# Graph layers on one core: marks for GpSimd written by ScalarE, the transposed mask taken as a sign, and two layernorm steps placed later

## The chip, the cores and the metric

The kernel runs on one core of one Trainium2 chip. The core has five engines that work side by side, each through its own queue in order: TensorE (PE, its weight loads shown as PEld), VectorE (DVE), ScalarE (ACT), GpSimd (POOL) and SyncE (SP), which issues DMAs. They wait for each other through semaphores. The metric is the device time of one execution in microseconds (us), lower is better.

## What is computed

The reference takes 16 graphs of 1024 nodes with 64 channels, a weighted adjacency matrix of 1024 x 1024 for each (its pattern of edges symmetric, about 16 neighbours in a row), and runs four layers with a layernorm and a ReLU ahead of each and a residual sum after it:

```python
h = relu(layernorm(x));  x = x + (tanh([h, adj @ h] @ W1 + b1) @ W2 + b2)        # layer 0
h = relu(layernorm(x));  x = x + ((adj + I) @ h) / (rowsum(adj) + 1)             # layer 1
h = relu(layernorm(x));  x = x + gin(h + quantiles(h, dilate(adj)))              # layer 2
h = relu(layernorm(x));  x = x + ((adj @ h) / colsum(adj)) @ Wn + h @ Ws + b     # layer 3
```

`dilate` drops from each row with more than 10 neighbours every skip-th one (counted along the row by a running sum), and the same edges in the transposed place; `quantiles` takes, per node and channel, a weighted sum of the 25%, 50% and 75% quantiles of the values of the neighbours that are left.

## The kernel before

Each graph goes through six streams of work, written as generators: `adjacency` (load rows, compare with zero, transpose, dilate, build a key per neighbour), `layers` (layers 0 and 1, the layernorm of layer 2), `neighbour_lists` (the columns of each node's neighbours, by repeated maxima), `gathers` (neighbours' rows of h into `raw`), `sorts` (a sorting network over `raw`, then the weighted sums) and `tail` (rest of layer 2, layer 3, output). Different graphs stand in different streams at the same time.

*The order of the work* is written by hand. A `Clock` carries planned times for VectorE, TensorE, ScalarE and GpSimd. A generator issues some instructions, adds their planned cost, and yields the planned time from which it wants to go on; the loop at the end of `direct_path` goes on with the first stream, in a fixed order of priority, whose time has come on VectorE's planned clock. So what is yielded sets only the place of the next instructions in each engine's queue. `after(dve, pe, act, lat)` adds the costs, ScalarE's after TensorE's after VectorE's, and gives back the end plus `lat`.

*Gathers and gates.* `gathers` (L1233 on) issues on GpSimd, per graph, 124 indirect DMAs (L1275), each of 128 rows of h, in five groups; each is planned at 1.39 us. At every fourth one it calls `gate()` and yields `clk.pool - 5`. `gate` (L914), if VectorE's planned clock is 3 us past the last mark, has VectorE write a mark (a memset of one element, L917), and GpSimd copy it (L919). GpSimd thereby waits for all that VectorE has in its queue up to there. A sort of a group (L1308) waits for its gathers; gathers into a group's buffer wait until the graph before has sorted it.

*The mask.* In `adjacency` each block of 128 rows is compared with zero (L942, `nb`, in f16, its diagonal taken out in L944) and is also transposed by TensorE into `adjt` (L949, L950), f32, which holds the whole transposed matrix with its diagonal. `flipped(i)` (L975) transposes `nb` once more, eight 128 x 128 tiles on TensorE into a PSUM bank of a ring of three (`bank()`), and ScalarE copies it out (L980). Running counts are products of that tile with a staircase (L991); ScalarE takes an absolute value (L995) and VectorE a comparison (L1000, L1005), which gives `gone`.

*Layernorm.* `preln` (L843) is called four times a graph. VectorE subtracts the mean, ScalarE squares (L851), VectorE sums the squares (L853), ScalarE takes the root (L854), VectorE the reciprocal (L856) and the product (L857), ScalarE the ReLU (L858). The places of L853 and L856 in VectorE's order come from the `lat` of the calls of `after` at L852 and L855, 1.2 and 1.5 us.

*Messages.* `messages` (L871) multiplies `adjt` with h, 32 products of 512 columns (L877), and ScalarE copies the result out (L878). In layer 1, eight ScalarE copies of `adjt` in place (L1212) follow, which sum it up for layer 3. The plan has 10.5 us of TensorE for the first (L1187) and 14.0 for the second (L1216), 1.1 us of ScalarE after each.

A flag of graphs that this path can't take (`bad`, L1455 on) sends all to another path; with these inputs it isn't taken.

Of the kernel before, what the change touches and what calls it, by code (L numbers as in the profile page):

```python
# [19 lines left out]
NB = 8  # L20
# [28 lines left out]
BIG = 1e30  # L49

E_ID, E_ONE, E_CAP, E_LOW, E_CN, E_HALF, E_Q, E_END = 0, 128, 256, 264, 272, 280, 288, 352
J_ID, J_BIG, J_OFF, J_ST, J_ROW, J_ONE, J_PI, J_NI, J_END = 0, 128, 256, 384, 896, 1920, 2048, 2176, 2184

# [678 lines left out]
def direct_path(ctx: ExitStack, tc: tile.TileContext, t: dict, out: bass.AP, flag):  # L732
# [17 lines left out]
    tt, ts, act = nc.vector.tensor_tensor, nc.vector.tensor_scalar, nc.scalar.activation  # L750
# [4 lines left out]
    ch = const.tile([P, J_END], F16, name="eh")  # L755
    nc.scalar.dma_start(ch, t["eh"])
    identf, onesf = cf[:, E_ID:E_ID + P], cf[:, E_ONE:E_ONE + P]
    cap8, low8, cn8, half8 = (cf[:, e:e + NB] for e in (E_CAP, E_LOW, E_CN, E_HALF))
    identh, big_i, offdiag = (ch[:, e:e + P] for e in (J_ID, J_BIG, J_OFF))
    stair, pidx = ch[:, J_ST:J_ST + N // 2], ch[:, J_PI:J_PI + P]  # L760
    nid = ch[:, J_NI:J_NI + NB]
    jrow, onerow = ch[0:1, J_ROW:J_ROW + N], ch[0:1, J_ONE:J_ONE + P]
    eps = const.tile([P, 1], F32, name="eps")
    nc.vector.memset(eps, 1e-5)
    bad = const.tile([P, NB], F32, name="bad")
    nc.vector.memset(bad, 0.0)

    def weight(name, n):
        w = const.tile([n, t[name].shape[1]], F32, name=name)
# [45 lines left out]

    clk = Clock()

    def after(dve=0.0, pe=0.0, act=0.0, lat=0.3):

        clk.dve += dve  # L820
        at = clk.dve
        if pe:
            clk.pe = at = max(clk.pe, at) + pe
        if act:
            clk.act = at = max(clk.act, at) + act
        return at + lat


    def bank(dt=F32):
        return psum.tile([P, 2048 // mybir.dt.size(dt)], dt, tag="t", name="pt", bufs=3)  # L830
# [12 lines left out]
    def preln(u, x, ha):  # L843

        s = nodes.tile([P, 4, NB], F32, name="stat")
        xc = mid(u, [P, NB, C])
        sq = mid(u, [P, NB, C])
        nc.vector.tensor_reduce(s[:, 0], x, AX.X, ALU.add)
        ts(s[:, 1], s[:, 0], 1.0 / C, None, op0=ALU.mult)
        tt(xc, x, s[:, 1, :, None].to_broadcast([P, NB, C]), ALU.subtract)  # L850
        act(sq, xc, AF.Square)  # L851
        yield after(1.5, act=0.65, lat=1.2)  # L852
        nc.vector.tensor_reduce(s[:, 2], sq, AX.X, ALU.add)  # L853
        act(s[:, 3], s[:, 2], AF.Sqrt, bias=eps, scale=1.0 / C)  # L854
        yield after(0.7, act=1.0, lat=1.5)  # L855
        nc.vector.reciprocal(s[:, 2], s[:, 3])  # L856
# [50 lines left out]
        return v.rearrange("c (q u p) -> c u q p", u=2, p=P)[:, u]  # L907


    marks = []  # L910
    slots = const.tile([1, 8], F32, name="mark")
    opened = const.tile([1, 2], F32, name="gate")

    def gate():  # L914
        if not marks or clk.dve > marks[-1] + 3.0:
            k = len(marks)
            nc.vector.memset(slots[:, k % 8:k % 8 + 1], 0.0)  # L917
            clk.dve += 0.15
            nc.gpsimd.tensor_copy(opened[:, k % 2:k % 2 + 1], slots[:, k % 8:k % 8 + 1])  # L919
            marks.append(clk.dve)  # L920


    state = [dict() for _ in range(B)]
    done = set()
    queued = []
# [9 lines left out]
    def adjacency(b):  # L935
        g = state[b]
        adjt = graph.tile([P, NB, N], F32, name="adjt")
        nb = graph.tile([P, NB, N], F16, name="nb")
# [32 lines left out]
        nc.vector.scalar_tensor_tensor(sf[:, 3], mn[:, 0], 2.0, sf[:, 2], op0=ALU.mult, op1=ALU.add)  # L971
        clk.dve += 0.9
        gone = graph.tile([P, NB, N], F16, name="gone")

        def flipped(i):  # L975
            nbt = lists.tile([P, NB, P], F16, name="nbt")
            p = bank(F16)
            for j in range(NB):
                nc.tensor.transpose(p[:, j * P:(j + 1) * P], nb[:, i, j * P:(j + 1) * P], identh)
            nc.scalar.copy(nbt, p.rearrange("p (j m) -> p j m", m=P))  # L980
            return nbt

        nbt = flipped(0)
# [1 line left out]
        for i in range(NB):  # L985
            following = flipped(i + 1) if i + 1 < NB else None

            p = bank2()
            for j in range(NB):
                o, e = j * P, (j // 4 + 1) * 512  # L990
                nc.tensor.matmul(p[:, o:e], nbt[:, j, :], stair[:, :e - o], start=j % 4 == 0, stop=j % 4 == 3)  # L991

            for q in range(2):
                s = slice(q * 512, (q + 1) * 512)
                act(gone[:, i, s], p[:, s], AF.Abs, bias=sf[:, 2 + q, i:i + 1], scale=2.0)  # L995
            nbt = following
            ready = after(0, pe=3.7, act=2.4, lat=3.0)
            if waiting:
                yield waiting[1]
                ts(gone[:, waiting[0], :], gone[:, waiting[0], :], sf[:, 1, waiting[0]:waiting[0] + 1], -1.0,  # L1000
                   op0=ALU.is_equal, op1=ALU.mult)
                clk.dve += 0.5
            waiting = (i, ready)
        yield waiting[1]
        ts(gone[:, waiting[0], :], gone[:, waiting[0], :], sf[:, 1, waiting[0]:waiting[0] + 1], -1.0,  # L1005
           op0=ALU.is_equal, op1=ALU.mult)
        clk.dve += 0.5
        keys_d = dram.tile([N, N], F16, name="keys_d")
        ms = nodes.tile([P, NB], F32, name="ms")
        for i in range(NB):  # L1010
# [16 lines left out]
            act(p, p, AF.Sign, accum_out=ms[:, i:i + 1])  # L1027
            yield after(0, pe=4.5, act=2.3) - 4.0

        mv = nodes.tile([P, NB], F32, name="mv")  # L1030
        act(mv, ms, AF.Copy, bias=512.0, scale=0.5)
        yield clk.act + 2.0
        key = nodes.tile([P, NB], F32, name="key")
        nc.vector.scalar_tensor_tensor(key, ms, 512.0, cn8, op0=ALU.mult, op1=ALU.add)
        neg = nodes.tile([P, NB], F32, name="neg")
        ts(neg, key, -1.0, None, op0=ALU.mult)
        p = bank2()
        for q in range(2):
# [5 lines left out]
        over = nodes.tile([P, NB], F32, name="over")  # L1044
# [7 lines left out]
        pi = nodes.tile([P, 2, NB], I32, name="pi")  # L1052
        ts(pi[:, 0], pos, P - 1, None, op0=ALU.bitwise_and)
        ts(pi[:, 1], pos, 7, None, op0=ALU.arith_shift_right)
        ph = nodes.tile([P, 2, NB], F16, name="ph")
# [3 lines left out]
        high = nodes.tile([P, NB, NB], F16, name="high")  # L1059
        tt(high, pidx[:, None, :NB].to_broadcast([P, NB, NB]), ph[:, 1, :, None].to_broadcast([P, NB, NB]),  # L1060
           ALU.is_equal)
        both = nodes.tile([P, 2, NB, NB], F16, name="both")
# [339 lines left out]
        done.add(("tail", b))  # L1402


    wcol = const.tile([P, 3], F32, name="wcol")
    for k, w in enumerate((0.25, 0.5, 0.25)):
        nc.vector.memset(wcol[:, k:k + 1], w)
    none = const.tile([P, 2], F32, name="none")
    nc.vector.memset(none[:, :1], BIG)
    nc.vector.memset(none[:, 1:], 0.0)  # L1410
    sizes = [max(p0 + ns * nn for l, p0, _, ns, nn in PACKS if l == k) for k in range(NPACK)]
# [43 lines left out]
                assert soonest is not None  # L1455
                clk.dve = soonest

    one = nodes.tile([P, 1], F32, name="one")
    nc.vector.tensor_reduce(one, bad, AX.X, ALU.max)
    p = bank()  # L1460
    nc.tensor.matmul(p[:1, :1], one, onesf[:, :1], start=True, stop=True)
    nc.vector.tensor_copy(flag, p[:1, :1])


@with_exitstack
# [10 lines left out]
def _constants():  # L1476

    import numpy as np

    p = np.arange(P)  # L1480
    ef = np.zeros((P, E_END), np.float32)
    ef[p, E_ID + p] = 1
    ef[:, E_ONE:E_ONE + P] = 1
    e = E_Q
    for b0, n, cap, low, *_ in GROUPS:
        ef[:, E_CAP + b0:E_CAP + b0 + n] = PLACES[b0:b0 + n]
        ef[:, E_LOW + b0:E_LOW + b0 + n] = low
# [9 lines left out]
    eh[p, J_BIG + p] = 2048  # L1497
    eh[:, J_OFF:J_OFF + P] = 1
# [81 lines left out]
```

## Time and profile before

| what | value |
|---|---|
| time, median of 3 runs (lowest to highest) | 3909.36 us (3884.14 to 3925.28) |
| the profiled execution: its own time, its span | 3897.33 us, 3895.5 us |
| mean granted TensorE clock | 0.689 |
| one gate of GpSimd, L919: number, mean | 477, 344 ns |
| sum of squares on VectorE, L853: number, mean | 64, 680 ns |
| reciprocal, L856: number, mean | 64, 196 ns |
| transposes of the mask, L979: number, busy | 1024, 99.8 us |
| products with the staircase, L991: number, mean | 1024, 365 ns |
| VectorE's first mark, last mark | 142.8 us, 3796.2 us |

The profile is of one execution. A line of a group gives the line of the kernel, engine and operation, what it writes <- what it reads, shapes and number, then the busy time in us and the mean of one in ns, then the time its engine sat idle just before these instructions and what ended most of that. A wait is put down to the instruction whose semaphore came last. "issue" is time for which the profile shows no releaser. Lines in order of time give start and duration in us, and in brackets the idle time of that engine before. Busy shares are averages over stages, and the last 400 us, with the last graphs alone, look unlike the rest.

### The profile page before, as it was taken

Reading aid. Unit: us, or ns where it says so; the run is one execution under the profiler, and the core shown is the slowest. Engines: PE = TensorE matmul, PEld = TensorE weight load, DVE = VectorE, ACT = ScalarE, POOL = GpSimd, SP = SyncE. Lnnn points to the kernel's source line nnn. Section 1 sums busy time; section 2 is a strip of 40 time slices with the busy share of each in tenths; the row PEclk is TensorE's granted clock in tenths of the full one; section 3 lists DMA queues with packets and bytes.
Section 4 is the critical chain, followed back from the end, with each engine's and each line's share of the span. In section 5 each row is a group of like instructions: output and inputs, shape, how many; then the busy total and the mean of one; then the engine's idle time right before and its main releaser. Section 6 shows DMA issues by size and latency. Waiting matters only on the chain.

```text
span 3895.5 us, 32579 instructions
## 1 busy us (share of the span) xinstructions
PE 2044.1 (52%) x8483; PEld 988.9 (25%) x8483; DVE 3035.7 (78%) x7309; ACT 1410.1 (36%) x2658; POOL 2644.1 (68%) x2792
## 2 busy tenths in 40 slices
PE   6464554646654574646446474565556555741113
PEld 3222222223222232222222232232222323220101
DVE  1557878879687897888787798899699876979482
ACT  5444334243433434333332443443344433430000
POOL 1077576776667686776776777777778686777781
PEclk8666667677676686676666777767677676765555
DMA  2313234152423425242341524243343423232121
GB/s 89 124 39 115 50 99 117 45 172 46 141 68 101 120 65 154 70 125 69 106 106 45 175 51 153 56 142 80 100 119 104 116 55 123 68 105 58 42 52 55
DMA packets 237348, 362.43 MB, mean 93 GB/s; under 512 B 126848, under 2 KB 128496, under 8 KB 237152
## 3 DMA queue, kind: packets, MB, share of 16 engines
q1 hardware_dynamic: 156912, 255.00, 19.0%
q0 software_dynamic: 80096, 104.70, 13.5%
q8 instruction: 69, 1.13, 0.1%
q14 instruction: 127, 1.04, 0.1%
q10 hardware_dynamic: 144, 0.56, 0.0%
HBM read 245.26 MB, written 114.81 MB: 92 GB/s over the span
## 4 chain that ended last, share of the span: by engine, by line
DVE 42%; issue 14%; PE 12%; another core or an unknown queue 9%; ACT 8%; POOL 8%; DMA 5%; SPq 0%; DVEq 0%; ACTq 0%; POOLq 0%
DVE other L1308 12%; DVE raw L1308 11%; POOL raw L1275 6%; PE pt L877 5%; DVE most L1117 4%; ACT adjt L1212 2%; DVE found L1103 2%; DVE agg L1327 2%; ACT sink L1047 2%; DMA k<-keys_d,node 1%; DMA raw<-h_d,index 1%; PE pt L901 1%; DVE k L1112 1%; DVE nb L942 1%
## 5 line engine op out<-in xcount | busy, mean ns | idle before, releaser
L1275 POOL DMA_INDIRECT raw<-h_d,index x1984 | 2148.8, 1083 | 559.0 <-issue 533.1
L1308 DVE TENSOR_TENSOR other<-raw 128x512 f32<-128x512 f32 (+11 forms) x816 | 536.7, 688 | 151.7 <-DMA raw<-h_d,index 113.9
L877 PE MATMUL pt<-adjt,ha 128*65 128x512 f32 (+1 forms) x1024 | 485.4, 635 | 44.6 <-DVE ha L1199 30.6
L919 POOL COPY gate<-mark 1x1 f32<-1x1 f32 x477 | 163.9, 344 | 416.2 <-DVE mark L917 369.3
L949 PE MATMUL pt<-ef,a 128*128 128x128 f32 x1024 | 207.5, 360 | 320.8 <-ACT adjt L950 129.6
L1308 DVE TENSOR_TENSOR raw<-other 128x512 f32<-128x512 f32 (+10 forms) x464 | 355.9, 792 | 5.8 <-DVE other L1308 0.6
L991 PE MATMUL pt<-eh,nbt 128*128 128x512 f16 (+3 forms) x1024 | 213.8, 365 | 266.5 <-ACT nbt L980 192.2
L1117 DVE MAX8 most<-k 128x8 uint16<-128x1024 uint16 x208 | 255.4, 1228 | 13.2 <-DVE k L1112 3.3
L949 PEld LDWEIGHTS pt<-ef,a 128*128 128x128 f32 x1024 | 157.7, 185 | 408.2 <-issue 180.6
L1024 ACT ACTIVATE nb<-pt 128x1024 f16<-128x1024 f32 x128 | 130.6, 1020 | 317.1 <-remote 118.4
L877 PEld LDWEIGHTS pt<-adjt,ha 128*65 128x65 f32 (+1 forms) x1024 | 148.1, 148 | 364.1 <-issue 360.1
L950 ACT COPY adjt<-pt 128x512 f32<-128x512 f32 x256 | 139.1, 583 | 250.0 <-remote 146.4
L956 ACT ACTIVATE nb<-nb 128x512 f16<-128x512 f16 x256 | 159.6, 629 | 179.3 <-DVE nb L942 70.2
L1308 DVE TENSOR_TENSOR raw<-other,raw 128x640 f32<-128x640 f32 (+3 forms) x448 | 216.5, 494 | 4.9
L1308 DVE TENSOR_TENSOR raw<-raw,other 128x128 f32<-128x128 f32 (+7 forms) x496 | 211.5, 436 | 6.1
L1020 PE MATMUL pt<-eh,gone 128*128 128x128 f16 x1024 | 129.7, 257 | 162.7 <-DVE gone L1000 76.5
L878 ACT COPY big<-pt 64x1024 f32<-64x1024 f32 (+1 forms) x32 | 32.2, 1007 | 496.1 <-PE pt L877 300.6
L1308 DVE TENSOR_TENSOR other<-other,raw 128x128 f32<-128x128 f32 (+4 forms) x448 | 201.4, 460 | 4.2
L1384 PE MATMUL tm<-at,ha 128*64 128x512 f32 x512 | 174.1, 785 | 50.0 <-DMA at<-adjt_d 44.4
L1103 DVE MAX8 found<-k 128x8 f32<-128x1024 f16 x128 | 156.3, 1221 | 51.2 <-DMA k<-keys_d,node 51.2
L991 PEld LDWEIGHTS <-nbt 128*128 128x128 f16 x1024 | 105.0, 116 | 359.4 <-ACT nbt L980 203.2
L1347 POOL DMA_INDIRECT res<-agg_d,pos x128 | 135.7, 1060 | 74.9 <-DMA agg_d<-agg 37.4
(182 smaller groups left out, 4350.6 us busy)
## 6 DMA issues: line engine op xcount, KB each, us to landing
a<-in_adj_dram SPq DMA_DIRECT2D x64, 1024.0 KB
adjt_d<-adjt SPq DMA_DIRECT2D x64, 1024.0 KB
at<-adjt_d SPq DMA_DIRECT2D x128, 512.0 KB
keys_d<-nb SPq DMA_DIRECT2D x64, 512.0 KB
raw<-h_d,index POOLq DMA_INDIRECT x1984
x<-in_x_dram SPq DMA_DIRECT2D x16, 256.0 KB
h_d<-h SPq DMA_DIRECT2D x16, 256.0 KB
agg_d<-agg SPq DMA_DIRECT2D x16, 256.0 KB
```

Of the source, the lines that this page charges most:

```text
L877: nc.tensor.matmul(p[p0:p0 + n, s], h[:, j, :n], adjt[:, j, s], start=j == 0, stop=j == NB - 1)
L919: nc.gpsimd.tensor_copy(opened[:, k % 2:k % 2 + 1], slots[:, k % 8:k % 8 + 1])
L949: nc.tensor.transpose(p[:, u * P:(u + 1) * P], a[:, j * P:(j + 1) * P], identf)
L950: nc.scalar.copy(adjt[:, 4 * q:4 * q + 4, i * P:(i + 1) * P], p.rearrange("p (u m) -> p u m", m=P))
L956: act(nb[:, i, s], nb[:, i, s], AF.Copy, accum_out=mn[:, q, i:i + 1])
L991: nc.tensor.matmul(p[:, o:e], nbt[:, j, :], stair[:, :e - o], start=j % 4 == 0, stop=j % 4 == 3)
L1103: nc.vector.max(out=found[:, o:o + 8], in_=src)
L1117: nc.vector.max(out=most, in_=less.bitcast(U16))
L1275: nc.gpsimd.indirect_dma_start(raw[:, s, i * C:(i + 1) * C], None, h_ds[b % 3], bass.IndirectOffsetOnAxis(ap=g["index"][:, at:at + 1], axi ...
L1308: tt(view(two[to], *((i, vi) if greater else (j, vj)), w), view(two[s], i, vi, w), view(two[u], j, vj, w), ALU.max if greater else ALU.min)
L1347: nc.gpsimd.indirect_dma_start(res[:, i, :], None, g["agg_d"], bass.IndirectOffsetOnAxis(ap=g["pos"][:, i:i + 1], axis=0))
L1384: nc.tensor.matmul(p[q * C:(q + 1) * C, :], ha[:, j, :], even(ats[j], q), start=j == 0, stop=j == NB - 1)
```

## The change

- The marks are written by ScalarE. `after`, when it plans ScalarE work, calls `mark()`: if ScalarE's planned clock is more than 3 us past the last mark, ScalarE copies one element into one of 32 slots. `gate()` writes no mark: it takes the newest mark whose planned end is more than 1 us before GpSimd's planned clock, and has GpSimd copy it, unless that mark has had its gate. VectorE's memset is gone.
- `flipped` is one ScalarE activation: the sign of 128 columns of `adjt`, with its sum to `signs`. The diagonal, which `adjt` holds, is taken off by one more product in each block, minus the identity with the staircase. The sums are compared with the counts at the end, so that a matrix with negative entries goes to the other path.
- In `preln` both `lat` become 4.0.
- Eight small tiles of `adjacency` and the flag's have one buffer instead of two, and six constant columns lie in one tile.

```diff
+    marks, gates = [], []
+    slots = const.tile([1, 32], F32, name="mark")
+    opened = const.tile([1, 2], F32, name="gate")
+    def mark():
+        if not marks or clk.act > marks[-1][0] + 3.0:
+            t = slots[:, len(marks) % 32:len(marks) % 32 + 1]
+            nc.scalar.copy(t, eps[:1])
+            clk.act += 0.2
+            marks.append((clk.act, t))
+    def gate():
+        due = [m for m in marks[-20:] if m[0] < clk.pool - 1.0]
+        if due and gates[-1:] != due[-1:]:
+            gates.append(due[-1])
+            nc.gpsimd.tensor_copy(opened[:, len(gates) % 2:len(gates) % 2 + 1], due[-1][1])
...
         if act:
             clk.act = at = max(clk.act, at) + act
+            mark()
         return at + lat
...
-        yield after(1.5, act=0.65, lat=1.2)
+        yield after(1.5, act=0.65, lat=4.0)
         nc.vector.tensor_reduce(s[:, 2], sq, AX.X, ALU.add)
         act(s[:, 3], s[:, 2], AF.Sqrt, bias=eps, scale=1.0 / C)
-        yield after(0.7, act=1.0, lat=1.5)
+        yield after(0.7, act=1.0, lat=4.0)
...
-    def gate():
-        if not marks or clk.dve > marks[-1] + 3.0:
-            k = len(marks)
-            nc.vector.memset(slots[:, k % 8:k % 8 + 1], 0.0)
-            clk.dve += 0.15
-            nc.gpsimd.tensor_copy(opened[:, k % 2:k % 2 + 1], slots[:, k % 8:k % 8 + 1])
-            marks.append(clk.dve)
...
+        signs = nodes.tile([P, NB], F32, name="signs", bufs=1)
         def flipped(i):
             nbt = lists.tile([P, NB, P], F16, name="nbt")
-            p = bank(F16)
-            for j in range(NB):
-                nc.tensor.transpose(p[:, j * P:(j + 1) * P], nb[:, i, j * P:(j + 1) * P], identh)
-            nc.scalar.copy(nbt, p.rearrange("p (j m) -> p j m", m=P))
+            act(nbt, adjt[:, :, i * P:(i + 1) * P], AF.Sign, accum_out=signs[:, i:i + 1])
             return nbt
...
-                nc.tensor.matmul(p[:, o:e], nbt[:, j, :], stair[:, :e - o], start=j % 4 == 0, stop=j % 4 == 3)
+                nc.tensor.matmul(p[:, o:e], nbt[:, j, :], stair[:, :e - o], start=j % 4 == 0,
+                                 stop=j % 4 == 3 and j != i)
+                if j == i:
+                    nc.tensor.matmul(p[:, o:e], minus_i, stair[:, :e - o], start=False, stop=j % 4 == 3)
...
+        tt(signs, signs, mn[:, 2], ALU.subtract)
+        tt(over_all, over_all, signs, ALU.add)
...
+    nc.vector.tensor_reduce(one[:, :1], over_all, AX.X, ALU.add)
+    ts(one[:, :1], one[:, :1], -1.0, float(B * NB), op0=ALU.mult, op1=ALU.add)
+    nc.vector.tensor_reduce(one[:, 1:], bad, AX.X, ALU.max)
+    tt(one[:, :1], one[:, :1], one[:, 1:], ALU.add)
```

More of the change, by code (lines that the diff above doesn't have):

```diff
@@ L51 @@
 E_ID, E_ONE, E_CAP, E_LOW, E_CN, E_HALF, E_Q, E_END = 0, 128, 256, 264, 272, 280, 288, 352
-J_ID, J_BIG, J_OFF, J_ST, J_ROW, J_ONE, J_PI, J_NI, J_END = 0, 128, 256, 384, 896, 1920, 2048, 2176, 2184
+J_ID, J_BIG, J_OFF, J_ST, J_ROW, J_ONE, J_PI, J_NI, J_NEG, J_END = 0, 128, 256, 384, 896, 1920, 2048, 2176, 2184, 2312
 PLACES = [21, 19, 17, 16, 15, 13, 12, 11]
@@ L758, in direct_path @@
     cap8, low8, cn8, half8 = (cf[:, e:e + NB] for e in (E_CAP, E_LOW, E_CN, E_HALF))
-    identh, big_i, offdiag = (ch[:, e:e + P] for e in (J_ID, J_BIG, J_OFF))
+    identh, big_i, offdiag, minus_i = (ch[:, e:e + P] for e in (J_ID, J_BIG, J_OFF, J_NEG))
     stair, pidx = ch[:, J_ST:J_ST + N // 2], ch[:, J_PI:J_PI + P]
@@ L762, in direct_path @@
     jrow, onerow = ch[0:1, J_ROW:J_ROW + N], ch[0:1, J_ONE:J_ONE + P]
-    eps = const.tile([P, 1], F32, name="eps")
+    cols = const.tile([P, 8], F32, name="cols")
+    eps, none, wcol = cols[:, :1], cols[:, 1:3], cols[:, 3:6]
     nc.vector.memset(eps, 1e-5)
@@ L766, in direct_path @@
     nc.vector.memset(bad, 0.0)
+    over_all = const.tile([P, NB], F32, name="over_all")
+    nc.vector.memset(over_all, 0.0)
     def weight(name, n):
@@ L907, in even @@
         return v.rearrange("c (q u p) -> c u q p", u=2, p=P)[:, u]
-    marks = []
-    slots = const.tile([1, 8], F32, name="mark")
-    opened = const.tile([1, 2], F32, name="gate")
-    def gate():
-        if not marks or clk.dve > marks[-1] + 3.0:
-            k = len(marks)
-            nc.vector.memset(slots[:, k % 8:k % 8 + 1], 0.0)
-            clk.dve += 0.15
-            nc.gpsimd.tensor_copy(opened[:, k % 2:k % 2 + 1], slots[:, k % 8:k % 8 + 1])
-            marks.append(clk.dve)
     state = [dict() for _ in range(B)]
@@ L1028, in adjacency @@
             yield after(0, pe=4.5, act=2.3) - 4.0
-        mv = nodes.tile([P, NB], F32, name="mv")
+        mv = nodes.tile([P, NB], F32, name="mv", bufs=1)
         act(mv, ms, AF.Copy, bias=512.0, scale=0.5)
         yield clk.act + 2.0
-        key = nodes.tile([P, NB], F32, name="key")
+        key = nodes.tile([P, NB], F32, name="key", bufs=1)
         nc.vector.scalar_tensor_tensor(key, ms, 512.0, cn8, op0=ALU.mult, op1=ALU.add)
-        neg = nodes.tile([P, NB], F32, name="neg")
+        neg = nodes.tile([P, NB], F32, name="neg", bufs=1)
         ts(neg, key, -1.0, None, op0=ALU.mult)
@@ L1043, in adjacency @@
                              start=True, stop=True)
-        over = nodes.tile([P, NB], F32, name="over")
+        over = nodes.tile([P, NB], F32, name="over", bufs=1)
         for i in range(NB):
@@ L1050, in adjacency @@
         ts(pos, over, 0.5, 511.5, op0=ALU.mult, op1=ALU.add)
-        pi = nodes.tile([P, 2, NB], I32, name="pi")
+        pi = nodes.tile([P, 2, NB], I32, name="pi", bufs=1)
         ts(pi[:, 0], pos, P - 1, None, op0=ALU.bitwise_and)
         ts(pi[:, 1], pos, 7, None, op0=ALU.arith_shift_right)
-        ph = nodes.tile([P, 2, NB], F16, name="ph")
+        ph = nodes.tile([P, 2, NB], F16, name="ph", bufs=1)
         nc.vector.tensor_copy(ph, pi)
@@ L1058, in adjacency @@
         tt(low, pidx[:, None, :].to_broadcast([P, NB, P]), ph[:, 0, :, None].to_broadcast([P, NB, P]), ALU.is_equal)
-        high = nodes.tile([P, NB, NB], F16, name="high")
+        high = nodes.tile([P, NB, NB], F16, name="high", bufs=1)
         tt(high, pidx[:, None, :NB].to_broadcast([P, NB, NB]), ph[:, 1, :, None].to_broadcast([P, NB, NB]),
            ALU.is_equal)
-        both = nodes.tile([P, 2, NB, NB], F16, name="both")
+        both = nodes.tile([P, 2, NB, NB], F16, name="both", bufs=1)
         tt(both[:, 0], high, nid[:, :, None].to_broadcast([P, NB, NB]), ALU.mult)
@@ L1402, in tail @@
         done.add(("tail", b))
-    wcol = const.tile([P, 3], F32, name="wcol")
     for k, w in enumerate((0.25, 0.5, 0.25)):
         nc.vector.memset(wcol[:, k:k + 1], w)
-    none = const.tile([P, 2], F32, name="none")
     nc.vector.memset(none[:, :1], BIG)
@@ L1456, in direct_path @@
                 clk.dve = soonest
-    one = nodes.tile([P, 1], F32, name="one")
-    nc.vector.tensor_reduce(one, bad, AX.X, ALU.max)
+    one = nodes.tile([P, 2], F32, name="one", bufs=1)
+    nc.vector.tensor_reduce(one[:, :1], over_all, AX.X, ALU.add)
+    ts(one[:, :1], one[:, :1], -1.0, float(B * NB), op0=ALU.mult, op1=ALU.add)
+    nc.vector.tensor_reduce(one[:, 1:], bad, AX.X, ALU.max)
+    tt(one[:, :1], one[:, :1], one[:, 1:], ALU.add)
     p = bank()
-    nc.tensor.matmul(p[:1, :1], one, onesf[:, :1], start=True, stop=True)
-    nc.vector.tensor_copy(flag, p[:1, :1])
+    nc.tensor.matmul(p[:1, :1], one[:, :1], onesf[:, :1], start=True, stop=True)
+    ts(flag, p[:1, :1], 1.0, None, op0=ALU.min)
 @with_exitstack
@@ L1497, in _constants @@
     eh[p, J_BIG + p] = 2048
+    eh[p, J_NEG + p] = -1
     eh[:, J_OFF:J_OFF + P] = 1
```

## The prediction

> **What bounds the kernel now.** I read the page first: no engine is full, so I went to the groups, then to the waits of GpSimd (POOL), then to the order of time around one of them.
>
> ```profile
> PE 2044.1 (52%) x8483; PEld 988.9 (25%) x8483; DVE 3035.7 (78%) x7309; ACT 1410.1 (36%) x2658; POOL 2644.1 (68%) x2792
> ```
>
> POOL's 68% is deceptive. The groups show why, and what the change touches:
>
> ```profile
> L1275 POOL DMA_INDIRECT raw<-h_d,index x1984 | 2148.8, 1083 | 559.0 <-issue 533.1 <-DVE mark L917 9.2 <-DVE other L1308 4.9
> L919 POOL COPY gate<-mark 1x1 f32<-1x1 f32 x477 | 163.9, 344 | 416.2 <-DVE mark L917 369.3 <-DVE den L1219 19.4 <-DVE other L1308 10.2
> L1212 ACT ACTIVATE adjt<-adjt 128x1024 f32<-128x1024 f32 x128 | 133.2, 1044 | 0.0
> L980 ACT COPY nbt<-pt 128x1024 f16<-128x1024 f16 x128 | 128.2, 1013 | 79.5 <-remote 54.8 <-PE pt L979 14.8 <-PE pt L991 4.7
> L917 DVE MEMSET mark<- 1x1 f32 x477 | 27.6, 59 | 0.0
> ```
>
> The 1984 gathers take 1083 ns each and 0.27 us of issue before each (533.1 / 1984), which nothing hides: 2682 us of the 3895.5. With the other row gathers, issue included (128 list loads 164, 128 result rows 173, 48 packed rows 82), and the gates' 164, POOL is occupied for about 3265 us between its first work at 143 and its last gather at 3808, 3665 us. What is left, some 400 us, is real waiting. VectorE is nearly as full: 3036 busy, and most of its 860 us idle has a releaser on another engine. So two in-order queues, each with some 10% of slack, are tied together.
>
> ```profile
> POOL gate L919 <- DVE mark L917: 369.3, 65, 124.5
> ...
> DVE stat L853 <- ACT mid L851: 96.3, 14, 16.8
> DVE stat L856 <- ACT stat L854: 64.3, 9, 19.0
> DVE gone L1000 <- ACT gone L995: 52.5, 10, 15.7
> ```
>
> The columns are total, times, longest. One of the 65 gate waits is the start (124.5). The others, 245 us, with 30 us put down to den and other, are **275 us of POOL waiting for VectorE's marks**. The order of time shows where one comes from:
>
> ```profile
> 1007.79 0.94 POOL L1275 DMA_INDIRECT raw<-h_d,index  x1 [0.30 <-issue]
> 1011.83 1.01 ACT L878 COPY big<-pt 65x1024 f32<-65x1024 f32 x1 [23.46 <-remote]
> ...
> 1021.06 0.62 ACT L851 ACTIVATE mid<-mid 128x512 f32<-128x512 f32 x1
> ...
> 1021.71 0.69 DVE L853 TENSOR_REDUCE stat<-mid 128x8 f32<-128x512 f32 x1 [16.81 <-ACT mid L851]
> 1022.32 0.20 DVE L1219 RECIPROCAL den<-pt 128x8 f32<-128x8 f32 x1
> 1022.34 0.06 DVE L917 MEMSET mark<- 1x1 f32 x1
> 1022.55 0.18 POOL L919 COPY gate<-mark 1x1 f32<-1x1 f32 x1 [13.81 <-DVE den L1219]
> ```
>
> ScalarE stood at L878 for the message matmuls, then ran eight L1212 (8.3 us), then the square that VectorE wanted. VectorE stood 16.8 us at the reduction, and POOL 13.8 us at its gate. The source is ScalarE being late; VectorE passes it on.
>
> **What the Trainium skill says.** "TensorE: Matmul & The Clock Gate", section "Architectural detail", has VectorE and ScalarE as strict FIFO queues: the lines above agree (the den whose input was ready stood behind the reduction). "ScalarE: Activation LUTs", section "What ACT_TABLE_LOAD costs", prices an ACTIVATE with immediates at 186 ns + 0.833 ns an element and lets neighbours overlap by 93 ns: 1039 ns for 1024 elements, against the 1044 of L1212; for one element 187 ns, where the trace's nearest is 163 (L1070, 8 elements). "SBUF — State Buffer", section "Who interferes with whom", has VectorE and GpSimd share one port pair; the gate's 344 ns mean over a minimum of 177 is consistent with that.
>
> **The change part by part** (against the profiled 3897.3, span 3895.5; the median of the runs is 3909, 12 more).
>
> 1. *Marks off VectorE.* 477 memsets at 59 ns: 28 us less of VectorE, none of them preceded by idle time. VectorE holds POOL for part of the time only, so I count 20.
>
> 2. *Marks on ScalarE.* `after` is called with ScalarE work 45 times a graph, 720 in all; the 3 us rule drops those planned closer, I take 500. At 0.16 to 0.19 us that is 80 to 95 us on an engine idle for 64% of the span; hidden, except where ScalarE is late already. A mark has 32 slots, so its wait for an old gate's read is long past. If the cover were gone, 3 marks in a late stretch cost 0.6 us of VectorE's stall each time.
>
> 3. *Fewer gates.* A gate is asked for at each fourth gather and once for the lists, 39 times a graph, 624. Now one is made only when a newer mark is due; with some 500 marks, many in pairs between two asks, I take 370 for 477. A gate costs 0.344 + 0.16 issue after it, less the 0.30 issue that a gather has anyway: 0.20 us. 107 x 0.20 = 21 us of POOL; the bounds are 0 (477 stay) and 50 (230 stay). A gate names ScalarE instead of VectorE, so a gather whose buffer VectorE last read may need a wait of its own; sequencer waits run ahead under the gather before, so I count 0, at worst 0.05 x 1984 = 99.
>
> 4. *What a gate waits for.* This decides. Before, VectorE's mark is written when the gate is planned, up to 5 us ahead of POOL's planned time (`yield clk.pool - 5`). Now the newest ScalarE mark older than 1 us is taken: 1 to about 6 us of margin, some 3.5 on average. Gates lose the stalls that VectorE has by itself, waiting for gathers (113.9) or lists (51.2), but a stall as at 1011 to 1022 stays: ScalarE passed nothing there either until 1021. I take 20 of the 275 us as saved, with +150 (ScalarE's lateness hits POOL more directly) and -200 (nearly all gone) as ends.
>
> 5. *Layernorm.* The reduction is placed 2.8 us later in VectorE's order, the reciprocal 2.5 us. They idle 120.5 us (17 waits) and 64.3 us (9 waits). At most 17 x 2.8 + 9 x 2.5 = 70 us is filled with sort steps. Waits shorter than that and the start, where nothing else is ready, take some away; I count 40. No DMA is issued in these steps; what they move later is ha, the h_d write behind it on SP and POOL's wait for it, three layernorms x 5.3 us a graph, hidden behind two graphs of gathers in flight (a graph takes about 230 us).
>
> 6. *The mask.* Per graph 64 PE transposes and 8 copies of 1013 ns go; 8 Signs from SBUF come, bounded by L1212 with its accumulator (successive starts 1.04 us apart) and by 1044 + 189 if the read doesn't overlap: +0.03 to +0.22 us each, 4 to 28 us on idle ScalarE. PE loses 99.8 us and gains 128 products of 365 ns, 47. ScalarE no longer waits 79.5 us before L980 for a PSUM bank or a transpose queued behind messages, so `gone` comes earlier: of L1000's 58.9 us of waits (some 30 in the first 82 us) I count 15 as saved. Next late there is L995 behind the products.
>
> 7. *Small things.* The added vector operations are 2 of about 0.17 us a graph, 5 us in VectorE, and three at the end, under 1. Fewer buffers for small tiles of one stream: 0, since graphs don't overlap in that stream.
>
> Sum: -20 -21 -20 -40 -15 +5 = -111, of which I let 100 through, since the two queues hide a little of each other: 3897 - 100 = 3797, and with the 12 us to the median **about 3810 us**.
>
> **Rivals.** *POOL is set free.* If ScalarE, idle 64%, passes its marks ahead of POOL, the 275 us of part 4 shrink to about 75 and VectorE's order runs beside: -200 -21 -20 -40 -15 +5, about 3620; VectorE's own 3008 busy and ScalarE-caused stalls stop that, so I put it at 3700. For it: a third of VectorE's idle time is waits for gathers and lists. Against: the big gate waits stand beside waits for ScalarE.
>
> *The waits only move.* POOL waits for ScalarE what it waited for VectorE, and the later reductions are themselves waited for: only gates and memsets are left, 41 us, less new ScalarE lateness: 3890. This is also the case that the larger delay does nothing, since most stalls are 5 to 19 us long and 2.8 doesn't reach ScalarE's recovery.
>
> *Slower: ScalarE's late mark holds POOL.* The mark after the second message product is planned 1.3 us after 14 us of PE, but lies in the queue behind L878 and eight L1212. The chain of work shows 15 to 16 us for the 32 products, then 1.0 + 8.3: 25 us for 15.3, ten late. The first product is 15.7 + 1.0 for 11.8, five late. Before, VectorE had 6 us of planned leave at the den. With a margin of 3.5 the gates would hold POOL 6 + 2 us a graph, 16 x 8 = 128, and those for the row copies as much again in part; the next sort waits for its gathers, since a graph's first sort starts right after them (in the order of time, the fifteenth graph's are issued by 3422.2, its sort starts at 3424.1). It decides when POOL's new waits pass the 100 us gained above, 6 us a graph. At 11 a graph it gives 3909 - 100 + 176, about 3985.
>
> **Chances.** Forecast 0.42 (own range 3765 to 3860), set free 0.21, only moved 0.20, slower 0.17. The range of 3690 to 3965 leaves out the better half of the second and the worse half of the fourth. A measurement of this kernel tells about 1% from no change, 39 us: faster by more 0.63, within 0.20, slower 0.17.
>
> **What would show it.** After the change: L917's group gone and some 500 copies of about 0.16 to 0.19 us on ScalarE; gates near 370, with their waits named for ScalarE and 200 to 280 us in all beside the start (under 100: the first rival; over 350: the last). The reduction's and reciprocal's idle together near 140 for 185. L980's waits gone, `gone` waits near 40, PE busy near 1990. If VectorE's waits for gathers rise over 200, the late mark is at work. The forecast is wrong if POOL's waits change by more than 80 us either way.

## The result and the profile after

The changed kernel took 4033.7 us in the median of 4 runs (4013.5 to 4047.1), the kernel before 3905.7 measured beside it: a ratio of 1.0346, with an interval of 1.0307 to 1.0386. It is 3.5 per cent slower, where 3810 us and a gain were forecast, and it lies beyond the upper end of the range, 3965. The profiled execution took 4047.1 us, with a span of 4045.3.

Its lines are numbered anew: the gathers are L1290, the gates L840, the marks L831, the sum of squares L878, the reciprocal L881, the product L882, the ReLU L883, the messages L902 and L903, the eight copies L1227, the den L1234. The *den* is VectorE's reciprocal of the row sums in layer 1. It reads what TensorE makes of the second messages (L1221), so it ends the chain ReLU, messages, row sums. The *packed rows* (L1271) are gathers whose index comes through DRAM (`pack_d`). First the busy line of the page, then some groups (busy us, mean ns, then idle time before and its releasers):

```profile
PE 2019.8 (50%) x7587; PEld 920.2 (23%) x7587; DVE 3034.8 (75%) x6868; ACT 1463.6 (36%) x3280; POOL 2561.1 (63%) x2685
```

```profile
L1290 POOL DMA_INDIRECT raw<-h_d,index x1984 | 2121.8, 1069 | 576.3 <-issue 566.0 <-ACT mark L831 5.9 <-DMA raw<-h_d,index 1.2
...
L990 ACT ACTIVATE nbt<-adjt 128x1024 f16<-128x1024 f32 x128 | 133.9, 1046 | 0.0
...
L840 POOL COPY gate<-mark 1x1 f32<-1x1 f32 x370 | 111.9, 303 | 380.8 <-ACT mark L831 368.1 <-issue 5.7 <-ACT raw L1266 2.9
L831 ACT COPY mark<-cols 1x1 f32<-1x1 f32 x494 | 86.1, 174 | 0.4
```

The counts and durations are those of the prediction: 494 marks of 174 ns, 370 gates, no wait in front of the sign. No engine does more work than before, except ScalarE by 54 us. All of the loss is waiting, and the waits (total, times, longest) show where:

```profile
POOL gate L840 <- ACT mark L831: 368.1, 56, 12.8
DVE den L1234 <- PE pt L1221: 242.3, 14, 23.2
POOL packed L1271 <- DMA pack<-pack_d: 208.6, 28, 22.1
DVE other L1323 <- DMA raw<-h_d,index: 160.0, 23, 18.0
...
DVE stat L873 <- DMA x<-in_x_dram: 104.2, 15, 9.9
...
DVE stat L881 <- ACT stat L879: 36.3, 9, 6.0
...
DVE stat L878 <- ACT mid L876: 26.5, 8, 16.4
```

Three of them are to be compared with the kernel before. Layernorm's two waits there (96.3 and 64.3) have shrunk to 26.5 and 36.3: what the larger delays were to do, they did. But the den, 64 us before (40.7 of it without a named releaser), now waits for TensorE in 14 graphs, 17 us each; and the packed rows, 52.2 before, wait 208.6. The waits also repeat: nearly every graph has the same ones. The order of time around one den:

```profile
1475.44 0.69 DVE L882 TENSOR_TENSOR mid<-mid,stat 128x512 f32<-128x512 f32 x1
...
1489.27 0.61 ACT L883 ACTIVATE ha<-mid 128x512 f32<-128x512 f32 x1
...
1489.94 15.48 PE L902 MATMUL pt<-adjt,ha 128*65 128x512 f32 x32 [17.65 <-ACT ha L883]
...
1505.46 1.01 ACT L903 COPY big<-pt 65x1024 f32<-65x1024 f32 x1 [15.57 <-PE pt L902]
...
1508.99 0.21 DVE L1234 RECIPROCAL den<-pt 128x8 f32<-128x8 f32 x1 [16.54 <-PE pt L1221]
...
1514.68 0.17 ACT L831 COPY mark<-cols 1x1 f32<-1x1 f32 x1
1514.99 0.18 POOL L840 COPY gate<-mark 1x1 f32<-1x1 f32 x1 [10.74 <-ACT mark L831]
```

Two readings offer themselves. The gate at 1514.99 stands 10.7 us for a mark that lies behind the eight copies: the late mark, as the last rival had it. And VectorE stands 16.5 us at the den, which comes soon behind the product of L882 in its queue, before the messages can be done: an order in which the chain ReLU, messages, row sums is not covered.

### The profile page after: what moved, and what is told of

Its sections match the earlier page's. It is cut to its first block, busy times and chain, and to the rows that moved or that the text cites. A ratio compares the mean times of both kernels' runs of the same rounds, so it can differ in the third digit from the quotient of the medians.

```text
span 4045.3 us, 30669 instructions
## 1 busy us (share of the span) xinstructions
PE 2019.8 (50%) x7587; PEld 920.2 (23%) x7587; DVE 3034.8 (75%) x6868; ACT 1463.6 (36%) x3280; POOL 2561.1 (63%) x2685
## 4 chain that ended last, share of the span: by engine, by line
DVE 28%; PE 17%; ACT 13%; another core or an unknown queue 12%; POOL 11%; issue 10%; DMA 8%; SPq 1%; POOLq 0%; DVEq 0%; ACTq 0%
POOL raw L1290 10%; PE pt L902 8%; DVE most L1132 5%; DVE other L1323 5%; DVE raw L1323 4%; ACT adjt L1227 3%; DVE found L1118 3%; DMA k<-keys_d,node 2%; ACT nb L1039 2%; ACT pt L1042 2%; DMA pack_d<-index 2%; ACT sink L1062 2%; DVE agg L1342 1%; DVE k L1127 1%
## 5 line engine op out<-in xcount | busy, mean ns | idle before, releaser
L1290 POOL DMA_INDIRECT raw<-h_d,index x1984 | 2121.8, 1069 | 576.3 <-issue 566.0
L902 PE MATMUL pt<-adjt,ha 128*65 128x512 f32 (+1 forms) x1024 | 500.3, 651 | 136.7 <-ACT ha L883 84.7
L1001 PE MATMUL pt<-eh,nbt 128*128 128x512 f16 (+3 forms) x1024 | 252.1, 399 | 388.8 <-ACT nbt L990 266.0
L840 POOL COPY gate<-mark 1x1 f32<-1x1 f32 x370 | 111.9, 303 | 380.8 <-ACT mark L831 368.1
L902 PEld LDWEIGHTS pt<-adjt,ha 128*65 128x65 f32 (+1 forms) x1024 | 151.3, 151 | 467.6 <-issue 355.6
L1103 POOL DMA_INDIRECT k<-keys_d,node x128 | 133.1, 1040 | 182.7 <-DVE node L1088 124.8
L1030 PE MATMUL pt<-nb,eh 128*128 128x512 f16 x256 | 127.4, 497 | 234.6 <-ACT pt L1042 197.0
L961 PEld LDWEIGHTS pt<-ef,a 128*128 128x128 f32 x1024 | 147.5, 177 | 416.5 <-issue 183.2
L1001 PEld LDWEIGHTS <-nbt 128*128 128x128 f16 x1024 | 115.4, 125 | 509.6 <-ACT nbt L990 280.7
L903 ACT COPY big<-pt 64x1024 f32<-64x1024 f32 (+1 forms) x32 | 32.3, 1008 | 497.3 <-PE pt L902 335.7
L1399 PE MATMUL tm<-at,ha 128*64 128x512 f32 x512 | 187.8, 834 | 45.8 <-DMA at<-adjt_d 41.8
L1008 ACT ACTIVATE gone<-pt,sf 128x512 f16<-128x512 f32 x256 | 160.0, 674 | 108.7 <-remote 37.2
```

Of the source, the lines that this page charges most:

```text
L902: nc.tensor.matmul(p[p0:p0 + n, s], h[:, j, :n], adjt[:, j, s], start=j == 0, stop=j == NB - 1)
L961: nc.tensor.transpose(p[:, u * P:(u + 1) * P], a[:, j * P:(j + 1) * P], identf)
L1103: nc.gpsimd.indirect_dma_start(k, None, g["keys_d"], bass.IndirectOffsetOnAxis(ap=g["node"][:, i:i + 1], axis=0))
L1290: nc.gpsimd.indirect_dma_start(raw[:, s, i * C:(i + 1) * C], None, h_ds[b % 3], bass.IndirectOffsetOnAxis(ap=g["index"][:, at:at + 1], axi ...
L1399: nc.tensor.matmul(p[q * C:(q + 1) * C, :], ha[:, j, :], even(ats[j], q), start=j == 0, stop=j == NB - 1)
```

## The experiments

The kernel before stood at two levels in them: an upper one, 3897 to 3912 us, which is also that of the result, and a lower one, 3664 to 3668 us. Ratios are always against the kernel before measured beside the run. The runs at the upper level carry the chip numbers 0 and 15, those at the lower 5, 1, 7 and 15; the result carries none. The number 15 stands at both, so it is not shown that the level goes with the chip. What differs between the levels can be seen, its cause not. In the kernel before at the upper level (before_again), TensorE has 56 gaps of over 1.5 us before its products without a releaser, 316 us in all; no run at the lower level has one. The page's shares of the chain of work that ended last show it too, first before_again, then the kernel with the mask alone at the lower level:

```profile
DVE 43%; issue 14%; PE 11%; another core or an unknown queue 10%; POOL 9%; ACT 7%; DMA 5%; DVEq 0%; SPq 0%; POOLq 0%; ACTq 0%
```

```profile
DVE 59%; issue 11%; POOL 11%; PE 8%; DMA 7%; ACT 3%; SPq 0%; DVEq 0%; POOLq 0%; ACTq 0%
```

### The parts alone

```diff
# marks_only: the kernel before with mark() in after(), gate() for the newest due mark
# mask_only: flipped() as the sign, minus_i product, signs, over_all
# ln_later_only:
-        yield after(1.5, act=0.65, lat=1.2)
+        yield after(1.5, act=0.65, lat=4.0)
...
-        yield after(0.7, act=1.0, lat=1.5)
+        yield after(0.7, act=1.0, lat=4.0)
# marks_and_mask: the changed kernel with lat=1.2 and lat=1.5
```

> The kernel before, with the marks and gates of the change alone. Late-mark theory (GpSimd waits for marks that stand in ScalarE's queue behind the copies after the second messages): this part carries the loss, 3990 to 4040 us, gate waits over 330 us beside the start. Layernorm theory (the later places of the reduction and the reciprocal put ReLU, messages and what follows behind the key steps of ScalarE): 3870 to 3920, gate waits 240 to 290. Mask theory (the sign and the added product reorder TensorE and ScalarE): 3870 to 3920 too.

> The mask as a sign alone (with the small tiles in one buffer), VectorE's marks and the old layernorm places. Late-mark and layernorm theories: 3870 to 3905, TensorE busy near 1990. Mask theory: 3960 to 4030.

> The kernel before with both delays of layernorm at 4.0 alone. Layernorm theory: 3980 to 4040, with den's wait for the row sums over 200 us in all and x waits of some 100 us. Late-mark and mask theories: 3850 to 3910, den near 65.

> The changed kernel with both delays of layernorm back at 1.2 and 1.5. Late-mark theory: the loss stays, 3990 to 4040. Layernorm theory: 3850 to 3910, den's wait near 65, gate waits under 290. Mask theory: 3980 to 4040.

These expectations name times at the upper level; the kernel before took 3664 us here, so only the ratios can be compared: 1.0056 (1.0039 to 1.0073), 1.0013 (1.0006 to 1.0021), 1.0030 (1.0017 to 1.0042) and 1.0061 (1.0044 to 1.0078). No part carries the loss; together they would lose 1.0 per cent. None gains anything either.

> The changed kernel, nothing altered, beside the kernel before. The four parts run so far cost 0.1 to 0.6 per cent against a kernel before of 3664 us, where the two kernels of the result stood at 3906 and 4034. If the loss belongs to the change itself (late marks, layernorm and mask adding up): about 1.0 per cent where the kernel before takes 3664 (3700 us), 3.5 per cent where it takes 3906. If it comes from the three parts together whatever the chip: 3.5 per cent in both places, 3790 us beside 3664.

> The kernel before, nothing altered, for its trace beside those of the parts. If the 240 us between 3906 and 3664 are TensorE's (its work ends later than its records show): the key steps, where ScalarE stands up to 20 us behind the recorded end of its products in the first trace, show under 4 us here. If they are GpSimd's: gathers under 1000 ns or issue under 450 us.

These two stood at the upper level: 4025 against 3912 us, 1.030 (1.024 to 1.036), and 3890 us for the kernel before. The gaps of TensorE are there, so whether the whole change costs 1.0 per cent at the lower level stayed open.

> The kernel before with the marks and the layernorm places of the change, its mask still through TensorE. Beside a kernel before of some 3906 us: if the mask's denser products are what TensorE answers with its long late ends in the key steps (13 to 15 us behind the record, twice a graph), the loss is gone: within 1 per cent, late ends as in the kernel before (median near 0). If late marks and layernorm make the loss, whatever the mask: 2 to 3.5 per cent. Beside a kernel before of some 3664 us: 0.6 to 1.0 per cent in either case.

> The changed kernel with VectorE's marks and gates as before. Beside a kernel before of some 3906 us: if the mask's products make the loss, 2 to 3.5 per cent, late ends in the key steps as in the changed kernel. If ScalarE's late marks make it, within 1 per cent, and GpSimd's gates wait under 300 us. Beside a kernel before of some 3664 us: 0.3 to 0.5 per cent in either case.

Both ran beside 3668 us, and the first was a surprise to both theories: marks and later layernorm together, without the mask, are 5.4 per cent slower (1.0539, 1.0521 to 1.0557) at 3868 us, where each alone costs 0.6 and 0.3. Mask and later layernorm cost 0.26 per cent (1.0016 to 1.0037). So the loss belongs to a pair, and not to the level or to the mask.

### Order, or what GpSimd waits for

The pair changes two things. It changes what a gate waits for, and it changes planned costs: a mark is 0.2 us of ScalarE in the plan for 0.15 of VectorE, and the delays are 4.0. The plan sets every place in every queue. The two come apart if the plan's numbers are kept and only the instructions changed.

```diff
# same_order_no_gates: the changed kernel without
-            nc.gpsimd.tensor_copy(opened[...], due[-1][1])
# same_order_vector_marks: the changed kernel; mark() plans 0.2 us, but issues nothing, and gate() has
+            nc.vector.memset(t, 0.0)
+            nc.gpsimd.tensor_copy(opened[...], t)
# old_order_scalar_marks: the changed kernel; marks on ScalarE, planned as VectorE's were
-            clk.act += 0.2
...
+        if not spent or clk.dve > spent[-1] + 3.0:
+            clk.dve += 0.15
+            spent.append(clk.dve)
```

> The changed kernel, nothing altered. The kernel before has shown two levels, 3906 and 3664 us, and marks with later layernorm lost 5.4 per cent at the lower one. Either theory below: beside a kernel before of 3664, about 4 to 5 per cent (3820 to 3860 us); beside 3906, 3.0 to 3.5 per cent.

> The changed kernel with every instruction in its place, but GpSimd copies no mark (370 copies fewer; ScalarE's marks stay). Late-mark theory (what GpSimd waits for makes the loss): the loss goes, within 1 per cent of the kernel before or faster, den's waits under 100 us. Order theory (the planner's order, in which the den stands some 8 us of VectorE's work behind its ReLU where the messages take 25 us): it stays, at least 2.5 per cent slower, den's waits for TensorE over 200 us.

> The changed kernel with every other instruction in its place, but each gate waits for a mark that VectorE writes at that point, as in the kernel before; ScalarE writes none. Late-mark theory: the loss goes, within 1 per cent. Order theory: it stays, 2.5 to 5 per cent slower, since the stall at the den is VectorE's own and now holds GpSimd as well.

> The order of the version without ScalarE's marks (sign mask, later layernorm, planned costs as with VectorE's marks), but with the marks written by ScalarE and the gates waiting for those. Late-mark theory: the loss is here, 2.5 per cent or more slower. Order theory: it is gone, between 1 per cent slower and 1 per cent faster.

All at the upper level. The changed kernel: 1.0335 (1.026 to 1.041). In its order with VectorE's marks: 1.0565 (1.049 to 1.064), 4126 us. In the order of no_marks, with ScalarE's marks: 1.0040 (1.0019 to 1.0060). The order makes the loss; in the changed kernel's order it is some 2 per cent faster with ScalarE's marks than with VectorE's. So the loss doesn't come from having ScalarE write the marks. How the order costs time isn't told yet. With VectorE's marks GpSimd stands at its gates too (369.3 us in all, 8 to 11 us of it in most graphs just behind the den, at which VectorE stood): GpSimd being held at a gate, by either engine, could be part of the loss. Without gates the kernel took 5051 us, 29 per cent more, a size that neither theory had (den's waits, 245.6 us, are what the order theory expected). The gates are worth far more than they cost, and this run tells nothing of the late mark.

> The kernel before with all its instructions in their places and its planned costs, but with the marks written by ScalarE and the gates waiting for the newest of them. The prediction's first, third and fourth part: 40 to 60 us faster, 1.0 to 1.5 per cent. Late-mark theory: 2 per cent slower or more. Order theory: within 1 per cent.

The same with the order of the kernel before, beside 3668 us: 1.0027 (1.0016 to 1.0039). That is 10 us slower, so ScalarE's marks gain nothing here. Its gates have little to win, as the waits show (the start's wait stands at the list loads here):

```profile
POOL gate L837 <- ACT mark L825: 77.8, 25, 11.2
```

Nor have VectorE's, in the order of the kernel before (the kernel with the mask alone): 188.8 us, of which the start is 122.4.

### The den's place

What is the order's fault? For each kernel, the durations of VectorE's instructions between the den and the layernorm product that stands nearest ahead of it were summed from the trace, over the fourth to the sixteenth graph. (Neighbours overlap a little in the records, so the time that they fill is somewhat less. Where the sum is under 3 us, the nearest product is another layernorm's.)

| kernel | VectorE's work ahead of the den, us | den's waits in the list, us | ratio |
|---|---|---|---|
| the order of the kernel before (mask_only) | 27 to 42 in ten graphs, 0.7 to 13.5 in three | 26.7 | 1.0013 |
| marks_and_mask | 33 to 53, 43.5 or 43.6 from the eighth graph on | 31.9 | 1.0061 |
| ln_later_only | 2 to 40, irregular | 59.0 | 1.0030 |
| second_delay_undone | 14.5 in all | 200.5 | 1.0494 |
| changed kernel (after_fourth) | 11.7 and 8.7 in turn | 231.6 | 1.0588 |

In after_fourth, messages and row sums take some 24 us from the product on. (In the order of time above it is 33: there the ReLU itself came 13 us after the product, behind two of ScalarE's key steps that had each idled 7 us without a named releaser.) So in the last two kernels the den must wait, and does, in every one of these graphs. The next runs shorten the chain, or move the den:

```diff
# half_messages, half_messages_old: messages() of the changed kernel and of the kernel before
+        top = NB if n == C else NB // 2
-        for j in range(NB):
+        for j in range(top):
# den_later: the changed kernel
-        yield after(0, pe=14.0, act=1.1) + 6.0
+        yield after(0, pe=14.0, act=1.1) + 14.0
# second_delay_undone: the changed kernel with lat=1.5 for the reciprocal
```

> The changed kernel in its own order, with only 16 of the 32 products of the second messages (half of the neighbours are left out of layer 1). Order theory: some 7.5 us come off the chain from ReLU to den in each graph, and 14 dens waited 17 us for it: about 105 us faster than the changed kernel, 0.3 to 1.2 per cent slower than the kernel before; den's waits 120 to 150 us. If the den's wait costs nothing, because GpSimd sets the period: still 2.5 per cent slower or more.

> The kernel before in its own order, with the same half of the second messages left out (half of the neighbours are left out of layer 1). Order theory: its dens seldom wait (65 us in all), so it gains at most 40 us, 0 to 1 per cent. If shorter messages are worth 100 us in any order: 2.5 per cent faster.

> The changed kernel with the den planned 8 us later (14.0 for 6.0 behind the second messages), which puts 12 to 37 us of VectorE's work between the ReLU's product and the den where the changed kernel has 9 and 12 in turn. Order theory: den's waits for TensorE fall under 100 us, and the time to within 1 per cent of the kernel before. Late-mark theory: 2.5 per cent slower or more, since the marks stand where they stood.

> The changed kernel, nothing altered. Order theory: beside a kernel before of some 3666 us, 4.5 to 5.8 per cent slower (3830 to 3880), as marks with later layernorm; so the shorter messages, 3770, have won some 100 us, and the later den, 3762, too. If the shorter messages won nothing: 3770 here as well. Beside a kernel before of some 3900 us: 3.0 to 3.5 per cent once more.

> The changed kernel with the reciprocal's delay back at 1.5 us (the reduction's stays at 4.0). In this order 14.5 us of VectorE's work stand between the ReLU's product and the den in every graph. Order theory: den's waits 10 to 13 us a graph, 140 to 180 us in all, and the loss smaller by 50 to 80 us than the changed kernel's in this call. If the den's place has no part in the loss: the same as the changed kernel within 1 per cent.

The changed kernel at the lower level, without TensorE's gaps, takes 3881 us, 1.0588 (1.0570 to 1.0606). Its waits there, and below them those of marks_and_mask, which loses 0.6 per cent:

```profile
POOL packed L1271 <- DMA pack<-pack_d: 242.3, 30, 21.7
DVE den L1234 <- PE pt L1221: 231.6, 14, 23.1
DVE other L1323 <- DMA raw<-h_d,index: 195.2, 22, 18.0
POOL gate L840 <- ACT mark L831: 168.0, 18, 15.6
```

```profile
POOL gate L840 <- ACT mark L831: 145.5, 38, 11.7
DVE den L1234 <- PE pt L1221: 31.9, 2, 27.5
```

The sums of the gates' waits are close, those of the den's are not. That speaks for the den, but the gates' waits differ in their place: in the changed kernel 159 of the 168 us are one wait of 9 to 16 us, behind the eight copies, in each of 13 graphs; in marks_and_mask the gates behind the copies wait 48 us in all.

With half of the second messages the changed kernel takes 3770 us (1.0287, 1.0269 to 1.0306), 111 us less, and its dens wait 137.9 us; 105 was expected. The same cut in the order of the kernel before wins 32 us (0.9915, 0.9895 to 0.9935). So what is taken off this chain comes out nearly whole in the one order, and for the smaller part in the other. But the mark behind the copies comes earlier with shorter messages as well: the gates' waits fell from 168.0 to 67.9 us, so this pair of runs can't tell the den from the gate. The chain of work of the changed kernel (start, duration) shows what its loop is:

```profile
1647.86 15.31 PE pt L902 x32
1663.19 1.01 ACT big L903
1664.20 8.32 ACT adjt L1227 x16
1673.39 0.96 POOL raw L1290
...
1708.01 0.94 POOL raw L1290
1709.29 4.63 DMA k<-keys_d,node
...
1765.52 4.29 DMA pack_d<-index
1769.88 2.09 SPq L1150
1772.51 2.60 DMA out_dram<-x
1775.12 3.38 DMA x<-in_x_dram
1778.53 0.70 DVE stat L873
...
1875.67 15.75 PE pt L902 x32
```

Between the copies and the gathers stand the mark and the gate, in pieces too short for this view. In the order of time the gate is

```profile
1672.73 0.18 POOL L840 COPY gate<-mark 1x1 f32<-1x1 f32 x1 [14.01 <-ACT mark L831]
```

So this loop is messages, copies, the mark's gate, 36 us of gathers, the lists on VectorE, then SP's queue, where a graph's rows of x come behind the packed index and the output of others, then the next layernorm: 227.8 us from one L902 to the next, each link waited for by the next. From the fourth den to the sixteenth a graph takes 229.6 us on average, for 210.5 in mask_only, so the whole loss arises in this repeating part. The den isn't a link of this chain, the late mark is. In marks_only and marks_and_mask, too, the chain goes from the copies to the mark, 14 times each, with hardly a loss, so a place in the chain alone proves nothing. The packed index and x, whose waits rose (from 52 and 24 us in the kernel before to 242 and 95 here), stand in this loop as well.

The den later (3762 us, 1.0262, 1.0245 to 1.0279) takes all of the den's waits away and 119 of the 216 us, not the whole as expected. Its sorts wait longer for gathers, and its gates nearly as long as before:

```profile
DVE other L1323 <- DMA raw<-h_d,index: 247.0, 25, 28.3
POOL gate L840 <- ACT mark L831: 143.4, 23, 13.1
```

What is left, 2.6 per cent, is also what the late-mark theory expected of this run. With the second delay undone (3848 us, 1.0494, 1.0476 to 1.0511) 33 us come back for the 50 to 80 expected, and den's waits fall to 200.5, not to 140 to 180. The direction fits; being within 1 per cent of the changed kernel, the run alone doesn't separate the two expectations. So about half of the loss goes when the den stands later. Since the plan then moves other work too, this is the worth of that order, and that of the den's place only as far as nothing else in it counts. The other half goes with the rest of the order; whether GpSimd's gate behind the copies makes it, or other places, was not separated.

## Why the prediction was wrong

*The step that failed* is in part 5: "what they move later is ha, the h_d write behind it on SP and POOL's wait for it, three layernorms x 5.3 us a graph, hidden behind two graphs of gathers in flight". It treats a larger delay as a shift of two steps in an order that otherwise stays. What is yielded decides which stream goes on next, and so all later places; with the marks' planned costs moved as well (parts 1 to 4 give that move no price), the plan fell into a pattern that repeats every second graph and puts the den 9 to 12 us of work behind its product. Neither the messages nor the den was among the followers that part 5 lists. Of the 216 us that the change costs in after_fourth, the parts alone explain 36 (1.0 per cent of 3665); the other 180 come only with the pair's order.

*Marks and gates (1 to 4).* Counts and durations were right. Their worth, -61 us, was not: with the order held, these parts measured +10 us (before_order_scalar_marks), where VectorE's gates wait some 65 us beside the start (mask_only, 188.8 less 122.4). The 275 us that I budgeted from came from the upper level, and how much of those is TensorE's gaps there isn't known. In the changed kernel the gate waits rose to 368 us, over the 350 that I had named as the last rival's sign; its other sign, over 200 us of VectorE's waits for gathers, did not come (160.0). The first sign can't carry its theory: at the lower level the same kernel has gate waits of 168.0 us and loses more, 5.9 per cent. The slack of "some 10%" that I gave both queues is POOL's; VectorE's 860 us are 22 per cent of the span.

*Layernorm (5).* The idle time in front of the two steps fell from 185 us to 75 (39.2 and 36.3 by the groups), more than to the 140 forecast. Nothing of it was won: alone, the later places cost 0.3 per cent for the 40 us gained in the sum. In the changed kernel, idle time that was filled in one place came back at the den.

*Mask (6).* PE's busy time fell to 2020, not 1990: the 128 added products took 51.8 us for the 47 counted, and L1001's took 399 ns for 365. L990's wait is gone, as forecast. The waits of `gone` did not fall: 56.3 us by ScalarE for 52.5. Alone the mask costs 5 us, where 15 were counted as saved.

*The rivals.* The slower one gave 3985 us by ScalarE's marks, which two runs show to be neither needed for the loss (same_order_vector_marks) nor enough for it (old_order_scalar_marks). That it came nearest is luck. The case that decided, a new order in which a hidden chain is no longer hidden, was not among them, and it should have been: a planner that sorts all work again by its numbers can land in such an order with any change of them.

*What stays open:* what TensorE's gaps at the upper level are, and why the change costs 5.9 per cent without them and 3.0 to 3.5 with them; and what makes the other half of the loss, GpSimd's gate behind the copies or other places of the order.

## What to carry to other kernels

Where a hand-made plan sets the order, a changed planned cost is a changed order: list, for each long chain through other engines, how much work of the waiting engine stands between its start and its end, before and after, and predict from that. Hold the plan's numbers fixed and change only the instructions (or the reverse) to tell a price from an order. A wait that is named for an engine says who came last, not what made it late.

## What the runs showed of the hardware

The same program stood at two levels 6.5 per cent apart (3906 us in the result, 3664 to 3668 at the lower level), with gathers of nearly equal length (1083 ns at the upper level; 1077 at the lower in ln_later_only, which issues the same ones) and a mean granted clock of 0.689 for about 0.70. The gaps of TensorE without a releaser are what sets the levels apart in the traces: 250 to 450 us in the runs with gates at the upper level, 654 us in 127 places in the run without gates, none at the lower. What sets the level isn't known; the chip's number alone doesn't.

Taking the 370 gates away made GpSimd's gathers shorter (1017 ns for 1069) and the kernel 29 per cent slower. Its list loads then waited 1457 us for VectorE, and ScalarE's key step 788 us without a named releaser. That may have to do with TensorE's gaps, since it was run at the upper level alone; why isn't shown.
